# A cross-attention layer on one core: the calls to all engines issued in a new order from a table

## The chip, the cores and the metric

The kernel runs on one core of a Trainium2 chip. A core has five engines that run their own instruction queues side by side: TensorE (PE, matrix products, with its weight loads shown as PEld), VectorE (DVE), ScalarE (ACT), GpSimd (POOL) and SyncE (SP, which here only issues DMA transfers; POOL issues some too, and ACT two at the start). Each queue is worked off in its order; an instruction that waits for another engine or for a transfer holds up all that stand behind it on the same queue. The metric is the device time of one execution in microseconds (us); the time given is the median over several runs.

## The reference

Cross attention with a layer norm ahead of it and a residual behind. The masked keys of a batch get no weight; all arrays are float32.

```python
# x: (8, 256, 1024), ctx: (8, 256, 1024), mask: (8, 256), Wq, Wout: (1024, 1024), 32 heads of 32
mu = jnp.mean(hidden_states, axis=-1, keepdims=True)
var = jnp.var(hidden_states, axis=-1, keepdims=True)
x = (hidden_states - mu) * jax.lax.rsqrt(var + LN_EPS) * ln_gamma + ln_beta
Q = _split_heads(x @ Wq.T)
K = _split_heads(memory_keys)        # the context
V = _split_heads(memory_values)      # the context again
scores = jnp.einsum('bhsd,bhtd->bhst', Q, K) * scale
scores = jnp.where(mask, scores, -jnp.inf)
probs = jax.nn.softmax(scores, axis=-1)
attn = jnp.einsum('bhst,bhtd->bhsd', probs, V)
out = attn @ Wout.T                  # after the heads are joined
return residual + out
```

## The kernel before

The work is cut into 64 steps n: step n is batch n // 8 and one chunk of 128 columns (four heads of 32) of that batch's 256 rows. The names in the code carry these numbers: sc_17_2 are the scores of step 17's third head, po_0_S1 a projection of batch 0, pq_21 the query chunk of step 21.

**A step.** PE multiplies the step's queries by its keys (`scores`, L654, eight calls into four PSUM banks named sc). DVE adds the mask bias mb (L644, one per batch) and takes the row maximum (L694, e and mn); ACT takes the exponential and the row sum (L698, den); DVE takes the reciprocal (L708, rden); POOL, or ACT for some heads, scales (L714 and L712). DVE transposes e in blocks of 32 by 32 into pT (L720), ACT copies a part aside (L726, pc), and four small transfers per step, in two pairs (pT<-pT, then pT<-pc, L800, on SP), swap blocks so that pT holds the transposed weights. PE multiplies these by the values v_all (L840, pv), for most steps a pair at a time, two and three steps after the scores. ACT copies the result into at (L853).

**The projections.** The query projection of the first batches goes chunk by chunk (`make_q`, L458 and L513, pq); from batch 3 on it is done by a scheme of seven products for a two-by-two block matrix (`query_product`, L615), and so is the output projection (`product_steps`, L930, into banks named po_..., with the product's name S1, S2, A11 and so on). The schemes need sums of blocks of weights and of data: of Wout (wo, L350), of Wq (wq, ring, L564), of the normalised x (sx, L603) and of the attention (at, s2, L906), nearly all on POOL. DVE gathers the products with L636 and L631 (into qa), L972 and L968 (into r). The layer norm's gamma is folded into each chunk of Wq on POOL (L534), with a layer norm by DVE (L399 to L425) and POOL (L407), and x is transposed by PE in batch 0 (px) and by DVE and small transfers later (xe, xnT).

**What sets the order.** The loop over n issues, per step: the scores of step n + 1, output projections, values, query projections, then the softmax of step n + 1 with loads and evacuations hooked in between, then statistics, sums and folds. Where each stands is written out in the code and in a table of slots (PLAN). The scheduler is set to manual, so that each engine's queue is in the order of the calls. A buffer or PSUM bank that is written again waits for its last reader, wherever that stands.

## Time and profile before

| what | value |
|---|---|
| time, median of 3 runs | 574.21 us (573.05 to 574.57) |
| the profiled execution, first to last instruction | 572.0 us |
| PE busy | 562.9 us, 98% |
| DVE busy | 466.2 us, 81% |
| ACT busy | 450.5 us, 79% |
| POOL busy | 399.1 us, 70% |
| transfers | 116.93 MB, mean 204 GB/s |

The profiled execution's span is 2.2 us shorter than the median of the runs; differences are made within the span. In rows in order of time the first number is the start, the second the duration; `x16` means sixteen records merged into one row, and the bracket says how long the engine was idle before it and what ended that. Each float32 matmul call of the program shows as two records. A row of the waits gives the total idle time, how often, and the longest. SPq is SP issuing a transfer; the duration there is that of the issue, and the landing comes later.

### The profile page before, as it was taken

The numbers are of one execution on the slowest core, as the hardware profiler recorded it, in microseconds if no ns is written. First come the engines' busy times: TensorE is split into PE (matmuls) and PEld (weight loads), VectorE is DVE, ScalarE is ACT, GpSimd is POOL, SyncE is SP. The second block draws the span as 40 slices with busy tenths as digits, with TensorE's granted clock in tenths as the row PEclk, the third lists the DMA queues.
The fourth block names the chain that finished last, engine by engine and source line by source line (L and its number), as shares of the span: only waits on it lengthen the run. The fifth ranks groups of instructions, "written<-read, shape, count | busy, mean of one in ns | idle before, by whom it ended". The sixth has DMA issues, their size and how long they took to land.

```text
span 572.0 us, 20001 instructions
## 1 busy us (share of the span) xinstructions
PE 562.9 (98%) x7162; PEld 394.6 (69%) x7162; DVE 466.2 (81%) x1701; ACT 450.5 (79%) x1527; POOL 399.1 (70%) x643
## 2 busy tenths in 40 slices
PE   8999999999999999999999999999999999999998
PEld 7788775767667677667675777667766777755454
DVE  5988899988878888988788987898877878688833
ACT  3699978888779877888768988789868888879920
POOL 1478978887678895787667774686955875267690
PEclk9999999999999999999999999999999999999999
DMA  8768778576777677877888677767866765547551
GB/s 298 278 174 252 203 206 230 133 205 189 203 235 203 205 207 220 257 210 205 214 249 234 206 201 221 229 200 209 233 189 193 226 182 175 145 136 228 153 167 74
DMA packets 45891, 116.93 MB, mean 204 GB/s; under 512 B 9136, under 2 KB 9904, under 8 KB 45792
## 3 DMA queue, kind: packets, MB, share of 16 engines
q1 hardware_dynamic: 38080, 90.14, 55.2%
q0 software_dynamic: 7424, 25.50, 15.1%
q8 instruction: 57, 0.93, 0.7%
q14 instruction: 42, 0.34, 0.2%
q10 hardware_dynamic: 288, 0.01, 0.0%
HBM read 64.23 MB, written 11.53 MB: 132 GB/s over the span
## 4 chain that ended last, share of the span: by engine, by line
PE 69%; DVE 9%; POOL 8%; ACT 6%; issue 4%; DMA 3%; SPq 0%; DVEq 0%; ACTq 0%; POOLq 0%
PE po_S L930 17%; PE pq_A L615 16%; PE sc L654 8%; PE pv L840 8%; PE po_A L930 8%; PE pq_S L615 6%; POOL e L714 5%; ACT e L698 3%; DVE e L694 3%; PE po_end L997 3%; DVE pT L720 3%; DMA pT<-pT 2%; ACT e L712 1%; PE pq L513 1%; DMA wq<-in_wq_dram 1%
## 5 line engine op out<-in xcount | busy, mean ns | idle before, releaser
L698 ACT ACTIVATE e<-e,mn 128x256 f32<-128x256 f32 x512 | 253.7, 502 | 32.8 <-DVE mn L694 30.2
L714 POOL TENSOR_SCALAR e<-e,rden 128x256 f32<-128x256 f32 x408 | 188.5, 476 | 125.0 <-DVE rden L708 116.8
L720 DVE STREAM_TRANSPOSE pT<-e 128x512 f32<-128x512 f32 x256 | 180.4, 707 | 54.6 <-POOL e L714 23.5
L694 DVE CUSTOM_DVE_ANT_0 e<-sc,mb 128x256 f32<-128x256 f32 x512 | 185.1, 415 | 13.0 <-PE sc L654 12.0
L726 ACT COPY pc<-pT 128x512 f32<-128x512 f32 x128 | 78.8, 617 | 43.7 <-DVE pT L720 28.5
L698 ACT ACTIVATION_READ_ACCUMULATOR e<-e,mn 128x1 f32 x512 | 98.9, 193 | 0.0
L513 PE MATMUL pq<-xnT,wq 128*128 128x256 f32 (+1 forms) x368 | 84.5, 383 | 0.0
L513 PEld LDWEIGHTS pq<-xnT,wq 128*128 128x128 f32 x368 | 68.6, 190 | 14.6 <-issue 3.4
L930 PE MATMUL po_S<-wo,at 128*128 128x512 f32 x152 | 73.5, 606 | 1.0 <-DVE r L972 0.7
L654 PE MATMUL sc<-k,qa 32*128 32x256 f32 x1024 | 73.8, 401 | 0.1
L654 PEld LDWEIGHTS sc<-k,qa 32*128 32x128 f32 x1024 | 45.9, 184 | 39.0 <-issue 17.8
L840 PE MATMUL pv<-pT,v_all 64*32 64x128 f32 x3584 | 61.0, 273 | 1.0 <-ACT e L712 0.6
L840 PEld LDWEIGHTS pv<-pT,v_all 64*32 64x32 f32 x3584 | 51.9, 105 | 12.8 <-issue 7.7
L930 PE MATMUL po_A<-wo,at 128*128 128x512 f32 x128 | 59.3, 604 | 0.1
L930 PE MATMUL po_S<-wo,s 128*128 128x512 f32 x104 | 49.9, 607 | 0.3 <-DVE rden L708 0.3
L708 DVE RECIPROCAL rden<-den 128x2 f32<-128x2 f32 x256 | 37.9, 148 | 13.1 <-ACT e L698 12.1
L712 ACT ACTIVATE e<-e,rden 128x256 f32<-128x256 f32 x104 | 46.8, 500 | 1.0 <-DVE rden L708 1.0
L615 PEld LDWEIGHTS pq_A<-xnT,wq 128*128 128x128 f32 x352 | 41.1, 192 | 5.6 <-issue 4.7
L930 PEld LDWEIGHTS po_S<-wo,at 128*128 128x128 f32 x152 | 26.0, 190 | 25.7 <-issue 23.9
L694 DVE DVE_READ_ACCUMULATOR2_ANT mn<- 128x1 f32 x512 | 42.3, 83 | 0.0
L615 PE MATMUL pq_A<-xnT,wq 128*128 128x128 f32 x352 | 41.2, 275 | 0.3 <-issue 0.3
L930 PEld LDWEIGHTS po_A<-wo,at 128*128 128x128 f32 x128 | 23.0, 189 | 26.5 <-issue 24.4
(116 smaller groups left out, 687.6 us busy)
## 6 DMA issues: line engine op xcount, KB each, us to landing
pT<-pT SPq DMA_DIRECT2D x128, 128.0 KB, 3.4
pT<-pc SPq DMA_DIRECT2D x128, 128.0 KB, 4.0
v_all<-in_kv_dram POOLq DMA_DIRECT2D x17, 512.0 KB, 4.8
k<-in_kv_dram SPq DMA_DIRECT2D x30, 256.0 KB, 4.2
r<-in_x_dram SPq DMA_DIRECT2D x26, 256.0 KB, 4.0
ring<-kept_T SPq DMA_DIRECT2D x11, 512.0 KB, 5.8
xnT<-xe SPq DMA_DIRECT2D x79, 64.0 KB, 3.9
out_dram<-r POOLq DMA_DIRECT2D x18, 256.0 KB, 3.7
```

The source lines that it names most:

```text
L513: nc.tensor.matmul(pqs[n], wq[:, o, c, :], xnTs[b](c), start=(c == 0), stop=(c == NC - 1),)
L615: nc.tensor.matmul(pqs[b][:, o, :], w[:, c], x_[:, c], start=begins and o + c == 0, stop=c == NK - 1, skip_group_check=True,)
L654: nc.tensor.matmul(scs[n][j][:, s, :], qa[r, n % NQ, ts(s, P)], ks[n - n % 2][r, n % 2, :], start=True, stop=True,)
L694: nc.vector.tensor_tensor_reduce(out=e[:, s, :], in0=pss[j][:, s, :], in1=mbs[n // NQ], scale=1.0, scalar=NO_SCORE, op0=ALU.add, op1=ALU.m ...
L698: nc.scalar.activation(e[:, s, :], e[:, s, :], AF.Exp, bias=mn[:, s : s + 1], scale=-1.0, accum_out=den[:, s : s + 1],)
L708: nc.vector.reciprocal(rden, dens[j])
L712: engine.activation(es[j][:, s, :], es[j][:, s, :], AF.Copy, scale=rden[:, s : s + 1])
L714: engine.tensor_scalar(es[j][:, s, :], es[j][:, s, :], rden[:, s : s + 1], 1.0, ALU.mult, ALU.mult,)
L720: nc.vector.transpose(pT[:, :, :, j, :, :].rearrange("p a i s k -> p (a i) s k"), es[j].rearrange("p s (b t) -> p b s t", t=K),)
L726: nc.scalar.copy(pc[:, :, ts(j, 2)], pT[:, 1, :, ts(j, 2)])
L840: nc.tensor.matmul(pvs[n][r][j * HD : (j + 1) * HD], vs[n - n % 2][ts(r, 2 * K), n % 2, i, ts(j, HD)], pT[ts(r, 2 * K), :, i, j, :, :], st ...
L930: nc.tensor.matmul(po, operand(b, name)[:, c], wo[:, which, c], start=begins and c == 0, stop=c == NK - 1, skip_group_check=not begins,)
```

## The change

The 6,932 calls on the engines are no longer issued when the code makes them. A wrapper around nc records each with its arguments, numbered in the old order, and at the end issues all in the order that a table (ORDER) lists. Each call stays on its engine and in its queue (OTHER, which could move one, is empty), buffers are still allocated while recording, and all engines' instruction counts are as before. What changes is who stands before whom in each queue: 1,875 of PE's 3,613 instructions have another place, 1,530 of DVE's 1,701, 904 of ACT's 1,017, 574 of POOL's 646, 446 of SP's 478. The mean move is 2 to 6 places, the largest 138 (DVE). In the changed kernel every instruction has the line of the issuing loop, L383.

```diff
+ORDER = """
+0-35 40 38 36-37 41 39 45 42-44 54-75 77 79-82 76 78 84-93 83 94-109 120-123 134 133 111-112 110 113 118
...
+"""
+OTHER = {}
...
+class Recorder:
+    def __init__(self, engine, calls):
+        self.engine, self.calls = engine, calls
+
+    def __getattr__(self, name):
+        return lambda *a, **k: self.calls.append((self.engine, name, a, k))
+
+
+class Recorded:
+
+
+    def __init__(self, nc):
+        self.nc, self.calls = nc, []
+        for engine in ("tensor", "vector", "scalar", "gpsimd", "sync"):
+            setattr(self, engine, Recorder(engine, self.calls))
+
+    def __getattr__(self, name):
+        return getattr(self.nc, name)
+
+    def issue(self, order, other):
+
+        done = set()
+        for run in order.split():
+            first, *last = map(int, run.split("-"))
+            for i in range(first, (last[0] if last else first) + 1):
+                engine, name, a, k = self.calls[i]
+                getattr(getattr(self.nc, other.get(i, engine)), name)(*a, **k)
+                done.add(i)
+        assert len(done) == len(self.calls)
...
     ctx.enter_context(tc.manual_schedule())
+    nc = Recorded(nc)
...
+    nc.issue(ORDER, OTHER)
```

Three places, as each engine's queue has them before and after. The last number of a name counts the tiles and differs between the two kernels.

**The head, SP.** The first loads before: x_0 and x_1 are the rows of batches 0 and 1 (four pieces of x_0), wq the chunks of Wq, mk_0 the mask, k_0 the keys.

```order
L259 DMA x_0_160<-in_x_dram 128x512 x4
L334 DMA wq_152<-in_wq_dram 128x1024
L259 DMA k_0_166<-in_kv_dram 128x512
L357 DMA mk_0_168<-in_mask_dram 128x512
L259 DMA x_1_170<-in_x_dram 128x1024
L334 DMA wq_152<-in_wq_dram 128x1024
L259 DMA x_1_170<-in_x_dram 128x1024
L334 DMA wq_152<-in_wq_dram 128x1024 x3
L259 DMA k_2_177<-in_kv_dram 128x512
```

And after:

```order
L383 DMA x_0_126<-in_x_dram 128x512 x2
L383 DMA mk_0_128<-in_mask_dram 128x512
L383 DMA wq_120<-in_wq_dram 128x1024
L383 DMA x_0_126<-in_x_dram 128x512 x2
L383 DMA x_1_129<-in_x_dram 128x1024
L383 DMA k_0_127<-in_kv_dram 128x512
L383 DMA wq_120<-in_wq_dram 128x1024 x2
L383 DMA x_1_129<-in_x_dram 128x1024
L383 DMA wq_120<-in_wq_dram 128x1024
```

The last two pieces of x_0 now stand behind the mask and the first chunk of wq, and two loads of wo and the values' first load stand between chunks of wq, which k_2 now follows.

**Around the scores of step 17, PE.** s2_0 and at_0_1 are the two halves' operands of the product S1 of batch 0, which go through the same bank one after the other. Before:

```order
L930 MATMUL po_0_S1_2306<-wo_157,s2_0_1607 128x512 x4
L513 MATMUL pq_21_2311<-xnT_2_1070,wq_152 128x256 x8
L930 MATMUL po_0_S1_2306<-wo_157,at_0_1_1162 128x512 x3
L654 MATMUL sc_17_0_2401<-k_16_1958,qa_151 128x256
L654 MATMUL sc_17_1_2402<-k_16_1958,qa_151 128x256
L654 MATMUL sc_17_2_2403<-k_16_1958,qa_151 128x256
L654 MATMUL sc_17_3_2404<-k_16_1958,qa_151 128x256
L654 MATMUL sc_17_0_2401<-k_16_1958,qa_151 128x256
L654 MATMUL sc_17_1_2402<-k_16_1958,qa_151 128x256
L654 MATMUL sc_17_2_2403<-k_16_1958,qa_151 128x256
L654 MATMUL sc_17_3_2404<-k_16_1958,qa_151 128x256
L930 MATMUL po_0_S1_2306<-wo_157,at_0_1_1162 128x512
```

And after (the first half's other two matmuls stand ahead of these rows):

```order
L383 MATMUL po_0_S1_598<-wo_125,s2_0_457 128x512 x2
L383 MATMUL pq_21_599<-xnT_2_340,wq_120 128x256 x6
L383 MATMUL sc_17_0_623<-k_16_539,qa_119 128x256
L383 MATMUL sc_17_1_624<-k_16_539,qa_119 128x256
L383 MATMUL sc_17_2_625<-k_16_539,qa_119 128x256
L383 MATMUL sc_17_3_626<-k_16_539,qa_119 128x256
L383 MATMUL sc_17_0_623<-k_16_539,qa_119 128x256
L383 MATMUL sc_17_1_624<-k_16_539,qa_119 128x256
L383 MATMUL sc_17_2_625<-k_16_539,qa_119 128x256
L383 MATMUL sc_17_3_626<-k_16_539,qa_119 128x256
L383 MATMUL pq_21_599<-xnT_2_340,wq_120 128x256
L383 MATMUL po_0_S1_598<-wo_125,at_0_1_355 128x512 x4
```

The scores have moved ahead of the second half. On DVE the call that empties the bank (r_0_1_1, L972) stood behind the first transpose of step 16 (pT_16) and now stands ahead of it.

**The query product of batch 3, PE and DVE.** pq_3_A11 is one product; its sums from wq and from ring use the same bank. PE before:

```order
L615 MATMUL pq_3_A11_2964<-sx_153,wq_152 128x128 x16
L930 MATMUL po_1_S2_2772<-wo_157,at_1_1_2329 128x512 x2
L654 MATMUL sc_23_0_3225<-k_22_2762,qa_151 128x256
L654 MATMUL sc_23_1_3226<-k_22_2762,qa_151 128x256
L654 MATMUL sc_23_2_3227<-k_22_2762,qa_151 128x256
L654 MATMUL sc_23_3_3228<-k_22_2762,qa_151 128x256
L654 MATMUL sc_23_0_3225<-k_22_2762,qa_151 128x256
L654 MATMUL sc_23_1_3226<-k_22_2762,qa_151 128x256
L654 MATMUL sc_23_2_3227<-k_22_2762,qa_151 128x256
L654 MATMUL sc_23_3_3228<-k_22_2762,qa_151 128x256
L615 MATMUL pq_3_A11_2964<-sx_153,ring_105 128x128 x16
```

And after (six more of the matmuls from wq, and two of po_1_S2, stand ahead of these rows):

```order
L383 MATMUL pq_3_A11_739<-sx_121,wq_120 128x128 x2
L383 MATMUL sc_23_0_784<-k_22_705,qa_119 128x256
L383 MATMUL sc_23_1_785<-k_22_705,qa_119 128x256
L383 MATMUL sc_23_2_786<-k_22_705,qa_119 128x256
L383 MATMUL sc_23_3_787<-k_22_705,qa_119 128x256
L383 MATMUL sc_23_0_784<-k_22_705,qa_119 128x256
L383 MATMUL sc_23_1_785<-k_22_705,qa_119 128x256
L383 MATMUL sc_23_2_786<-k_22_705,qa_119 128x256
L383 MATMUL sc_23_3_787<-k_22_705,qa_119 128x256
L383 MATMUL pq_3_A11_739<-sx_121,wq_120 128x128 x8
L383 MATMUL po_1_S2_708<-wo_125,at_1_1_605 128x512 x2
L383 MATMUL pq_3_A11_739<-sx_121,ring_105 128x128 x16
```

The scores of step 23 have moved from behind the last matmul from wq into the midst of these. DVE before, at the call that gathers the product (qa):

```order
L708 RECIPROCAL rden_22_1_3191<-den_22_1_3168 128x2
L720 STREAM_TRANSPOSE pT_22_3153<-e_22_0_3155 128x8x64
L708 RECIPROCAL rden_22_2_3196<-den_22_2_3175 128x2
L720 STREAM_TRANSPOSE pT_22_3153<-e_22_1_3166 128x8x64
L708 RECIPROCAL rden_22_3_3202<-den_22_3_3186 128x2
L720 STREAM_TRANSPOSE pT_22_3153<-e_22_2_3173 128x8x64
L636 TENSOR_TENSOR qa_151<-pq_3_A11_2964,qa_151 128x4x128
L720 STREAM_TRANSPOSE pT_22_3153<-e_22_3_3184 128x8x64
```

And after:

```order
L383 RECIPROCAL rden_22_1_780<-den_22_1_772 128x2
L383 RECIPROCAL rden_22_2_781<-den_22_2_775 128x2
L383 STREAM_TRANSPOSE pT_22_765<-e_22_0_767 128x8x64
L383 ISA e_23_0_790,mn_23_0_791<-sc_23_0_784,mb_2_591 128x256
L383 ISA mn_23_0_791 128x1
L383 STREAM_TRANSPOSE pT_22_765<-e_22_2_773 128x8x64
L383 ISA e_23_2_796,mn_23_2_797<-sc_23_2_786,mb_2_591 128x256
L383 ISA mn_23_2_797 128x1
L383 ISA e_23_0_790,mn_23_0_791<-sc_23_0_784,mb_2_591 128x256
L383 ISA mn_23_0_791 128x1
L383 TENSOR_TENSOR qa_119<-pq_3_A11_739,qa_119 128x4x128
```

Ahead of qa stand now three passes of step 23's scores and two transposes of step 22; two transposes have moved behind it. Further ahead, among the score passes of step 22, DVE has the sum wq<-wq that stood after step 23's before, and it waits for a POOL sum there.

On SP's queue in steps 3 to 5, of the two loads of wo that stood between the two pairs of swaps of pT_4 one stands in the head now and one behind the swaps of pT_5; two loads of v_all, the later of which waits for the values of step 2, stand ahead of the second pair of swaps of pT_3. On POOL, folds of wq and sums of wo stand earlier between the scalings of steps 5 to 13; the fold of the last chunk of wq has a sum of wo (which stood behind it) ahead of it. At the end of the kernel the values of steps 62 and 63 follow some 5 us more of other matmuls.

## The prediction, written before the changed kernel ran

> **What bounds the kernel now.** I read the page's busy times first, then the stages, then the list of who waited for whom, and only then the order in time at the places where the waits stood. The page's two rows that matter are:

> ```profile
> PE 562.9 (98%) x7162; PEld 394.6 (69%) x7162; DVE 466.2 (81%) x1701; ACT 450.5 (79%) x1527; POOL 399.1 (70%) x643
> L714 POOL TENSOR_SCALAR e<-e,rden 128x256 f32<-128x256 f32 x408 | 188.5, 476 | 125.0 <-DVE rden L708 116.8
> ```

> TensorE is busy 98% of the span; POOL idles 125 us ahead of its scalings, some 2 us in each of 64 steps. The view by stage (span of the stage, then PE's busy time, and later the granted clock):

> ```profile
> 0.00:16.40 16.40, 13.73 (x101) 12.00 (x101) 10.31 (x30) 7.26 (x20) 2.19 (x11) 1.00 0.86 311
> 16.40:140.00 123.60, 122.61 (x1473) 91.88 (x1476) 109.04 (x407) 107.67 (x361) 99.57 (x143) 1.00 0.72 204
> 140.00:230.00 90.00, 89.33 (x1133) 62.86 (x1128) 75.82 (x271) 70.95 (x241) 68.83 (x105) 1.00 0.75 212
> 230.00:480.00 250.00, 248.43 (x3378) 177.78 (x3363) 210.19 (x778) 205.37 (x706) 179.88 (x304) 1.00 0.76 216
> 480.00:538.00 58.00, 57.90 (x807) 34.61 (x813) 45.70 (x178) 49.70 (x172) 30.82 (x57) 1.00 0.60 166
> 538.00:572.00 34.00, 30.84 (x324) 15.45 (x308) 15.12 (x40) 9.52 (x32) 17.85 (x25) 1.00 0.39 117
> ```

> PE is idle 16.40 − 13.73 = 2.7 us in the head and 3.2 us in the last stage, and 0.99 + 0.67 + 1.57 + 0.10 = 3.3 us in all the 521.6 us between. The clock is 1.00 throughout, so it has nothing to give back. An order that leaves the matmuls as they are can win only these idle times. Who ended them:

> ```profile
> PE pq_A L615 <- issue: 1.3, 2, 1.0
> PE pq L458 <- DMA wq<-in_wq_dram: 1.0, 1, 1.0
> PE po_S L930 <- DVE r L972: 0.7, 1, 0.7
> PE pv L840 <- ACT e L712: 0.6, 1, 0.6
> PE po_S L930 <- ACT ends L948: 0.3, 1, 0.3
> PE po_S L930 <- DVE rden L708: 0.3, 1, 0.3
> PE pv L840 <- DMA v_all<-in_kv_dram: 0.2, 1, 0.2
> ```

> The two "issue" gaps lie inside one query product each, with fewer matmul records there than the program has matmuls; I take them for missing records and no idle time. The other rows after the head, with one more of 0.2, sum to 2.3 us in six stalls. The true loss is a little more: a matmul's record outlasts the moment at which the next may start, so that each stall hides some 0.13 us; 2.3 + 6 × 0.13 = 3.1 us. That is all that lies in mid-kernel.

> **The change part by part.** It adds and removes nothing: each engine issues as many instructions as before, and no switch between matmul shapes is added (scores stay in groups of 8, values in their groups). PE's work is therefore costed at nothing, and every term is a stall that goes or comes.

> *The wo loads step out of pT_4's swaps.* Before:

> ```profile
> 57.69 1.12 SPq L259 DMA_DIRECT2D wo<-in_woT_dram  x2
> 58.92 1.15 SPq L800 DMA_DIRECT2D pT<-pc  x2
> 67.85 0.61 PE L840 MATMUL pv<-pT,v_all 64*32 64x128 f32 x19 [0.61 <-ACT e L712]
> ```

> The wait is booked to ACT's e, which had long been done; the values of step 4 need the swapped block, whose second pair was issued behind 1 MB of wo. Without that MB (half of it is loaded in the head now, half after pT_5's swaps, both well ahead of wo's use) the swap lands in time, and this stall (0.6, or 0.7 from start to start) goes.

> *The evacuation before the second half of po_0_S1.* Before:

> ```profile
> 144.53 3.62 PE L513 MATMUL pq<-xnT,wq 128*128 128x256 f32 x16
> 148.11 0.65 DVE L972 TENSOR_TENSOR r<-po_S,r 128x512 f32<-128x512 f32 x1
> 148.81 0.70 PE L930 MATMUL po_S<-wo,at 128*128 128x512 f32 x1 [0.67 <-DVE r L972]
> ```

> The bank must be emptied (0.65 us on DVE) before PE writes it again. DVE's queue held that call behind a transpose; now it stands before the transpose, and PE has scores of 17 (some 1.1 us) among its work in between. This stall, the largest, goes: 0.8.

> The other four (v_all of step 6 is loaded earlier, the end's evacuations have more PE work ahead of the next use) make up the rest. Removed in all: −3.1, with the ends −3.1 and −1.5 (only these two).

> *The head.* SP's queue loads the second half of x_0 behind the mask and the first 512 KB of wq; before, it stood ahead of both. The rows of before, with the traffic between 2.5 and 8.5 us:

> ```profile
> 7.85 0.69 DVE L399 BATCH_NORM_STATS2 st<-x 128x6 f32<-128x512 f32 x1 [0.19 <-DMA x<-in_x_dram]
> 9.24 2.02 PE L458 MATMUL pq<-xnT,wq 128*128 128x128 f32 x16 [1.04 <-DMA wq<-in_wq_dram]
> 9.91 0.80 DVE L425 TENSOR_SCALAR x<-x,mv,rstd 128x1024 f32<-128x1024 f32 x1
> 15.72 0.31 PEld L654 LDWEIGHTS sc<-k,qa 32*128 32x128 f32 x8 [0.48 <-ACT qa L462]
> 2.50:8.50 6.00, 5.51 (x36) 5.04 (x34) 3.81 (x7) 1.98 (x3) 0.58 (x1) 1.00 0.95 299
> ```

> 576 KB at 299 GB/s are 1.9 us; the transfers overlap, so x_0's end comes 1.1 to 1.9 us later, and the chain statistics, norm (9.91), transposes, projection, scores (15.72) with it. Against that, wq comes as much earlier, and the wait of 1.04 at 9.24 goes: PE can do the first half's projection while it waits for the second half. DVE also has two statistics of x_1 (0.69 each) before the copies of x_0. From −1.0 (only the wq wait moves) to +1.9 (the whole delay). I take +0.75, above the middle, since the second half feeds the chain that ends last in this stage.

> *pT_3's second pair of swaps* now stands behind two loads of v_all, the later of which waits until the values of step 2 have read their buffer.

> ```profile
> 49.97 1.15 SPq L800 DMA_DIRECT2D pT<-pc  x2
> 52.09 1.16 PE L840 MATMUL pv<-pT,v_all 64*32 64x128 f32 x64
> 59.63 0.63 PE L840 MATMUL pv<-pT,v_all 64*32 64x128 f32 x26
> pT<-pc SPq DMA_DIRECT2D x128, 128.0 KB, 4.0
> pT<-pc SPq DMA_DIRECT2D x3, 128.0 KB, 7.0
> ```

> So it is issued at 52.09 + 1.16 + one load's issue (0.5), about 53.8 to 54.9 instead of 49.97 to 51.1. A swap lands after 4.0 us in the page's median and after 7.0 in the crowded stretch from 56 to 69 us. The block is wanted at 59.63: 58.9 is in time, 61.9 is 2.3 too late. There is less traffic now that wo has gone elsewhere, so I stay near the low end: +0.4 (0 to +2.3). Behind this wait on SP stand pT_4's swaps, issued from 56.2 on before; they are not reached.

> *POOL's fillers* (folds of wq, sums of wo) move ahead of scalings. Their cover is POOL's idle time above. Where there is none is the last fold:

> ```profile
> 84.53 1.90 POOL L534 TENSOR_TENSOR wq<-wq,gs 128x1024 f32<-128x1024 f32 x1
> 86.38 1.28 POOL L350 TENSOR_TENSOR wo<-wo 128x512 f32<-128x512 f32 x1
> 86.48 0.51 PEld L513 LDWEIGHTS pq<-xnT,wq 128*128 128x128 f32 x3 [0.38 <-POOL wq L534]
> ```

> The fold ends at 86.43, 0.05 us before its use. The sum of 1.28 behind it now stands ahead of it, inside step 8's scalings: 0 if those scalings wait less than they did, +1.2 if not. I take +0.3, by the 2 us that POOL idles in a step.

> *Query products.* In batch 3 the scores of 23 move out from between two groups of pq_3_A11 that share a bank:

> ```profile
> 202.88 1.88 PE L930 MATMUL po_S<-wo,at 128*128 128x512 f32 x4
> 204.44 0.65 DVE L636 TENSOR_TENSOR qa<-pq_A,qa 128x512 f32<-128x512 f32 x1
> 205.77 0.49 PE L615 MATMUL pq_A<-sx,ring 128*128 128x128 f32 x2
> ```

> PE left the bank at 202.88 and came back at 205.77. Now only the projection's matmuls are in between (202.88 to 204.70: 1.8), and DVE's sum of 0.65 must fit: room 1.8 − 0.65 = 1.2. DVE began it 204.44 − 202.88 = 1.6 late before, which would now cost 0.4. The queue order gives DVE two transposes ahead of it instead of three, but three score passes too. Batches 5 and 7 have the same gap, 4 and 6 a longer one. I take +0.3 for the three (0 to 3 × 0.4 = +1.2).

> The rest of the moved calls I cost at nothing. What hides them is that a step's values are computed two or three steps after its scores, which the order keeps: from 230 to 480 us PE lost 1.57 us, 1.3 of them the issue gaps, though the swaps, loads and evacuations of 30 steps were queued there. Where that cover is gone, a late pair of swaps costs what pT_3's does.

> Sum: −3.1 + 0.75 + 0.4 + 0.3 + 0.3 = −1.35, against 572.0 of span. The median of the runs, 574.21, is 2.2 above the span, which I leave: 574.21 − 1.35 = 572.9, say **572.8**. Its own range is 571.1 (the head at −1.0, the rest as taken) to 574.5 (only the two large stalls gone).

> **Rivals.** *Everything gained, nothing paid:* the wq wait gives 1.0 in the head and no new stall comes: 574.2 − 3.1 − 1.0 = 570.1. For it: PE's idle time in the head; against it: the x_0 chain. *Even:* the toll is twice what I took (2 × 1.75 = 3.5) and the gain 3.1: 574.6, within the ±0.3% (±1.7 us) that a measurement of this kernel can tell from no change. For it: 98% busy leaves nothing else.

> *Slower:* DVE held up by POOL at the query products. Two sums of the same form on DVE, and POOL beside the slow one:

> ```profile
> 142.14 1.32 POOL L564 TENSOR_TENSOR ring<-wq 128x512 f32<-128x512 f32 x1
> 142.26 1.75 DVE L564 TENSOR_TENSOR ring<-wq 128x512 f32<-128x512 f32 x1
> L564 DVE TENSOR_TENSOR wq<-wq x2: 650/664/678, 160.7 to 213.9; 128x512 f32<-128x512 f32 x2
> ```

> Beside POOL's sum the 0.65 became 1.75, 1.1 more; the new order puts one such sum (213.9 before) ahead of step 22's reciprocals, where it waits for POOL and meets its sums. If DVE is as late at pq_A as before (1.6) and 1.1 more, PE waits 2.7 − 1.2 = 1.5; with the same lateness in batches 3, 5 and 7, 4.5, and so 572.8 − 0.3 + 4.5 = 577.0. It decides from the point where DVE is over 1.2 us late. Against it: DVE idles ahead of the same sum now. [...]

> **How the numbers follow.** Forecast 0.48, half of it beyond the bound (0.24 faster, 0.24 same); everything gained 0.13; even 0.08; slower 0.31, in which I count pT_3's swaps at their upper end too. Faster 0.24 + 0.13 = 0.37; same 0.32; slower 0.31. The range goes from 570.0, the full gain, to 578.0, the slower rival's 577.0 with a little of a late fold; it leaves about 0.15 out.

> **What would show it.** Right: no wait of po_S for r L972 near 148 and none of pv near 67; PE's first unbroken stretch beginning 0.5 to 1 us later than 16.4; pq at 86 waiting for wq under 0.5. Wrong: a wait of pv near 60 for pT<-pc over 1 us; pq_A waiting for qa in batches 3, 5, 7; idle time on PE between 230 and 480 above 2 us, where I expect no new wait; or a switch of shape costing more in another neighbourhood, seen as PE busy above 563.

## The result, and the profile after

The changed kernel takes 581.91 us (median; 580.96 to 584.02) against 574.15 (573.05 to 574.57): a ratio of 1.0157, 95% interval 1.0126 to 1.0187. It is slower, by more than the forecast's range allowed. The profiled execution spans 579.3 us against 572.0, 7.3 more, and the working below is made on these two. One run of e1 (712.28 us, at a mean granted clock of 0.754) is left out of the figures below. The page of after, its busy times:

```profile
PE 565.7 (98%) x7162; PEld 400.4 (69%) x7162; DVE 459.6 (79%) x1701; ACT 451.8 (78%) x1527; POOL 402.0 (69%) x643
```

The view by stage, cut as in the prediction (the last stage is longer now):

```profile
0.00:16.40 16.40, 10.90 (x61) 10.50 (x62) 7.51 (x16) 3.52 (x7) 2.19 (x11) 0.90 0.85 301
16.40:140.00 123.60, 123.60 (x1417) 92.26 (x1415) 107.88 (x417) 108.72 (x364) 106.64 (x148) 1.00 0.72 209
140.00:230.00 90.00, 90.00 (x1146) 64.91 (x1146) 74.46 (x272) 70.60 (x237) 60.92 (x95) 1.00 0.75 209
230.00:480.00 250.00, 245.27 (x3393) 177.38 (x3392) 202.24 (x757) 203.18 (x697) 173.37 (x297) 1.00 0.74 210
480.00:538.00 58.00, 57.46 (x724) 35.85 (x728) 46.53 (x177) 47.22 (x164) 35.88 (x61) 1.00 0.63 181
538.00:579.30 41.30, 38.42 (x430) 19.53 (x424) 20.98 (x67) 18.50 (x63) 22.98 (x33) 1.00 0.37 108
```

PE is idle 16.40 − 10.90 = 5.5 us in the head (2.7 before), not at all from 16.4 to 230 (1.7 before), 4.7 from 230 to 480 (1.6 before), 0.5 to 538 (0.1) and 2.9 at the end (3.2). That is 4.5 more in all, and PE is busy 565.7 − 562.9 = 2.8 longer for the same matmuls: together the 7.3. Two stages got worse and the one between them got better. Who ended the waits:

```profile
PE pq L383 <- DVE xnT L383: 2.8, 1, 2.8
PE pq_A L383 <- issue: 2.2, 2, 1.2
PE pv L383 <- DMA pT<-pc: 1.7, 3, 0.9
PE busy L383 <- POOL ring masks.py:199: 1.3, 1, 1.3
PE pq L383 <- DMA wq<-in_wq_dram: 1.3, 1, 1.3
PE sc L383 <- DMA k<-in_kv_dram: 0.8, 1, 0.8
```

The waits of po_S for r, of pv for ACT's e, for v_all and so on are gone, as forecast. In their place stand x_0's copies in the head, the swaps of pT and a load of keys.

To see where the time is lost, I take each matmul call's start in a trace and subtract the time at which it would start if every call took as long, up to the start of the next, as in the kernel before. This "lag" is my own working from two traces, one execution of each kernel; it rises where PE loses time and falls where a stall of before is missing. The kernels of this document that are told apart by it (the edits of e1 to e16 are given with the experiments):

| lag in us at | 20 | 220 | 240 | 360 | 480 | 560 |
|---|---|---|---|---|---|---|
| after | 4.6 | 2.2 | 5.1 | 5.1 | 7.0 | 7.0 |
| e1 (x_0 first) | 1.3 | −0.9 | 2.0 | 1.7 | 5.1 | 4.9 |
| e8 (copies first) | 2.3 | 0.1 | 4.6 | 5.8 | 7.4 | 7.1 |
| e7 (PE kept busy in the head) | 3.1 | 0.7 | 3.4 | 4.2 | 8.3 | 8.4 |
| e15 (old order, first twelve loads new) | 2.1 | 6.5 | 6.5 | 5.5 | 9.2 | 9.1 |
| e11 (first twelve loads as before) | 0.3 | −1.3 | 1.2 | 0.8 | 3.7 | 3.4 |
| e9 (as e11 up to step 21, then the old order) | 0.0 | −2.4 | −2.4 | −2.0 | −1.7 | −1.7 |
| e10 (as e11, swaps in pairs) | 0.3 | −1.6 | 1.0 | 0.6 | 6.6 | 7.2 |
| e16 (as e11, three late places mended) | 0.3 | −1.7 | 3.2 | 2.9 | 6.7 | 7.3 |
| e13 (as e11, ScalarE's copies early) | 0.2 | −0.5 | −0.4 | 4.1 | 15.2 | 18.9 |

After loses 4.6 us by 20 us, wins 2.4 back up to 220, and loses 4.8 from there on, 2.9 of them between 220 and 240.

**The head.** The first statistics of x_0's second half on VectorE (DVE) in before:

```profile
6.97 0.69 DVE L399 BATCH_NORM_STATS2 st<-x 128x6 f32<-128x512 f32 x1
```

The rows of after in order of time, DVE first:

```profile
10.07 1.36 DVE L383 BATCH_NORM_STATS2 st<-x 128x6 f32<-128x512 f32 x2 [3.25 <-DMA x<-in_x_dram]
...
11.83 0.41 DVE L383 TENSOR_SCALAR xnT<-px,gam,bet 128x128 f32<-128x128 f32 x1
12.77 0.73 DVE L383 TENSOR_SCALAR xnT<-px,gam,bet 128x128 f32<-128x128 f32 x2 [0.53 <-ACT xnT L383]
```

and PE:

```profile
9.51 0.91 PE L383 MATMUL pq<-xnT,wq 128*128 128x128 f32 x6 [1.33 <-DMA wq<-in_wq_dram]
13.23 2.50 PE L383 MATMUL pq<-xnT,wq 128*128 128x128 f32 x10 [2.82 <-DVE xnT L383]
15.53 1.38 PE L383 MATMUL px<-ring,x 128*128 128x128 f32 x8
16.84 0.71 PE L383 MATMUL sc<-k,qa 32*128 32x256 f32 x8
```

The statistics of x_0's second half begin at 10.07, in before at 6.97. In DVE's queue the copies of the *first* half (xnT<-px), whose transposes PE ended near 8.2 us, stand behind those statistics, so that they too begin only at 11.83, and PE, which could have projected the first half, waits 2.82 us. The three copies stood behind the statistics before, too, but their own order is new: the one that PE needs next was the first of them and is now the second, behind another and behind a copy of ACT's from the same px (12.28 to 12.73), for which DVE waits 0.53 us. From the first copy's start to PE's next matmul it takes 13.23 − 11.83 = 1.40 us. In e15, which has these loads with the old order of the copies, it takes 0.47 (11.19 to 11.66). So some 0.9 of the 2.82 us come from the order of the copies. Then the matmuls run slowly: ten in 2.50 us. The clock in the view by stretches of 2 us:

```profile
12.00:14.00 2.00, 0.77 (x3) 0.77 (x4) 1.47 (x5) 0.46 (x1) 0.85 (x3) 0.70 1.02 406
14.00:16.00 2.00, 2.00 (x12) 2.00 (x11) 1.62 (x3) 0.22 (x1) 0.00 (x0) 0.50 1.03 400
16.00:18.00 2.00, 2.00 (x19) 1.50 (x18) 1.05 (x4) 1.54 (x5) 0.00 (x0) 0.94 1.05 394
```

By the trace's clock records the granted clock is 0.50 from 12.81 us, near the end of the wait, to 16.23. In before it was 1.00 in every stretch of 2 us up to 570, where PE's last matmul was over.

**After 220 us.** SP's queue, whose rows give the issue, and PE:

```profile
223.51 4.12 SPq L383 DMA_DIRECT2D pT<-pc  x2
227.67 0.98 SPq L383 DMA_DIRECT2D k<-in_kv_dram  x1
...
231.12 0.51 SPq L383 DMA_DIRECT2D pT<-pT  x1
231.68 0.58 SPq L383 DMA_DIRECT2D pT<-pc  x1
```

```profile
231.37 1.78 PE L383 MATMUL sc<-k,qa 32*128 32x256 f32 x16 [0.83 <-DMA k<-in_kv_dram]
235.19 1.25 PE L383 MATMUL pv<-pT,v_all 64*32 64x128 f32 x64 [0.95 <-DMA pT<-pc]
```

The load of k_26 is issued at 227.67 behind swaps (218.89 before). The last swap of pT_23 is issued at 231.68 behind a swap of the *next* step; the copy that feeds it had ended at 219.4. In the old order each step's four swaps stand in two unbroken pairs ahead of the next step's; in the new one 20 of 64 steps have a swap behind the next step's first, and 19 have one to seven other transfers inside the second pair. The life of two steps, from the traces (us):

| step | | last score | last transpose | last copy | last swap issued | values begin |
|---|---|---|---|---|---|---|
| 23 | before | 205.8 | 213.4 | 214.1 | 223.2 | 230.2 |
| 23 | after | 204.6 | 217.8 | 219.4 | 232.3 | 235.2 |
| 44 | before | 384.2 | 392.2 | 392.8 | 399.3 | 417.2 |
| 44 | after | 386.7 | 400.2 | 408.0 | 415.0 | 421.7 |

From the last score to the last swap it took 17.4 and 15.1 us before, and takes 27.7 and 28.3 now: every engine on the way hands on later. From the last swap's issue to the values there were 7 and 18 us; 3 and 7 are left, with a wait of PE in them both times.

The two steps are ones at whose values PE waits. By the same working for steps 24 to 59, the median from the last score to the last swap is 14.7 us before and 23.1 after, and from there to the values 12.5 and 6.8. Less than 5 us are left in none of these 36 steps before, in 13 of them after, and in none in e9, which has the old order there. In steps 4 to 19 the median has shrunk as much, from 12.9 to 6.5, and PE loses nothing there.

### The profile page after: what moved, and what is told of

It is laid out like the page before. It is cut to its first block, busy times and chain, and to the rows that moved or that the text cites. A ratio compares the mean times of both kernels' runs of the same rounds, so it can differ in the third digit from the quotient of the medians.

```text
span 579.3 us, 19950 instructions
## 1 busy us (share of the span) xinstructions
PE 565.7 (98%) x7162; PEld 400.4 (69%) x7162; DVE 459.6 (79%) x1701; ACT 451.8 (78%) x1527; POOL 402.0 (69%) x643
## 4 chain that ended last, share of the span: by engine, by line
PE 71%; DMA 9%; DVE 7%; ACT 4%; issue 3%; SPq 3%; POOL 2%; DVEq 0%; POOLq 0%; ACTq 0%
PE pq L383 15%; PE po_S L383 13%; PE sc L383 9%; PE pv L383 9%; PE pq_A L383 8%; PE po_A L383 7%; PE pq_S L383 5%; DMA pT<-pc 4%; DMA pT<-pT 3%; SPq L383 3%; ACT e L383 3%; PE po_end L383 3%; DVE e L383 2%; DVE pT L383 2%; POOL e L383 2%
## 5 line engine op out<-in xcount | busy, mean ns | idle before, releaser
L383 ACT ACTIVATE e<-e,mn 128x256 f32<-128x256 f32 x512 | 256.1, 503 | 43.5 <-DVE mn L383 33.3
L383 POOL TENSOR_SCALAR e<-e,rden 128x256 f32<-128x256 f32 x408 | 191.9, 482 | 131.3 <-DVE rden L383 126.8
L383 DVE STREAM_TRANSPOSE pT<-e 128x512 f32<-128x512 f32 x256 | 176.9, 702 | 32.7 <-POOL e L383 22.6
L383 DVE CUSTOM_DVE_ANT_0 e<-sc,mb 128x256 f32<-128x256 f32 x512 | 192.8, 411 | 12.2 <-PE sc L383 6.6
L383 ACT ACTIVATION_READ_ACCUMULATOR e<-e,mn 128x1 f32 x512 | 97.5, 190 | 0.0
L383 PE MATMUL pq<-xnT,wq 128*128 128x256 f32 (+3 forms) x400 | 92.7, 380 | 4.2 <-DVE xnT L383 2.8
L383 ACT COPY pc<-pT 128x512 f32<-128x512 f32 x128 | 77.3, 613 | 21.8 <-DVE pT L383 12.9
L383 PEld LDWEIGHTS pq<-xnT,wq 128*128 128x128 f32 x400 | 72.7, 194 | 23.2 <-issue 8.9
L383 PE MATMUL sc<-k,qa 32*128 32x256 f32 x1024 | 75.7, 401 | 0.8 <-DMA k<-in_kv_dram 0.8
L383 PE MATMUL po_S<-wo,at 128*128 128x512 f32 x152 | 72.6, 597 | 0.0
L383 DVE RECIPROCAL rden<-den 128x2 f32<-128x2 f32 x256 | 37.6, 153 | 43.3 <-ACT e L383 42.0
L383 PEld LDWEIGHTS sc<-k,qa 32*128 32x128 f32 x1024 | 47.8, 184 | 27.7 <-issue 14.3
L383 PE MATMUL pv<-pT,v_all 64*32 64x128 f32 x3584 | 60.7, 273 | 1.8 <-DMA pT<-pc 1.4
L383 PE MATMUL po_A<-wo,at 128*128 128x512 f32 x128 | 61.2, 602 | 0.0
L383 PEld LDWEIGHTS pv<-pT,v_all 64*32 64x32 f32 x3584 | 51.4, 105 | 13.4 <-issue 7.8
L383 ACT ACTIVATE e<-e,rden 128x256 f32<-128x256 f32 x104 | 49.2, 502 | 6.3 <-DVE rden L383 5.9
L383 PEld LDWEIGHTS pq_A<-xnT,wq 128*128 128x128 f32 x352 | 42.9, 192 | 12.3 <-issue 10.6
L383 PE MATMUL po_S<-wo,s 128*128 128x512 f32 x104 | 50.4, 601 | 0.0
L383 PE MATMUL pq_A<-xnT,wq 128*128 128x128 f32 x352 | 44.4, 277 | 1.2 <-issue 1.2
L383 DVE DVE_READ_ACCUMULATOR2_ANT mn<- 128x1 f32 x512 | 42.4, 83 | 0.0
L383 ACT COPY at<-pv 128x128 f32<-128x128 f32 x128 | 30.5, 252 | 13.9 <-PE pv L383 13.9
L383 PEld LDWEIGHTS po_S<-wo,at 128*128 128x128 f32 x152 | 26.1, 191 | 18.7 <-issue 18.3
## 6 DMA issues: line engine op xcount, KB each, us to landing
pT<-pT SPq DMA_DIRECT2D x128, 128.0 KB, 3.3
pT<-pc SPq DMA_DIRECT2D x128, 128.0 KB, 3.6
```

The costliest lines, as they stand in the source:

```text
L383: getattr(getattr(self.nc, other.get(i, engine)), name)(*a, **k)
```

## The experiments

Ratios are to the kernel before, run on the same chip. Each kernel is the changed one with its table edited. The numbers are those of calls: 34 to 37 are x_0's loads, 38, 42 and 44 to 46 wq, 39 k_0, 40 the mask, 41 and 43 x_1.

### The head mended in three ways

e1 puts x_0's second half back behind the first:

```diff
-0-35 40 38 36-37 41 39 45 42-44 54-75 77 79-82
+0-37 40 38 41 39 45 42-44 54-75 77 79-82
```

> The new order with one edit on SP's queue: the last two pieces of x_0 again right behind the first two, ahead of the mask and the first piece of wq. Theory A (the head's loss is this load: x_0's second half lands 2 us late, DVE's queue holds the copies of the first half behind its statistics, PE idles 2.8 us and then runs 1.4 us longer at a lower clock): about 4.5 us less than the new order, 577.4, with pq_0 waiting under 0.5 us and the clock at 1.00 from 12 to 18 us. Theory B (the pace is set by the other engines' chains, so what the head gives is waited away at the first late swap): less than 1.5 us gained, 580.5 or more, with longer waits of pv in steps 3 to 10.

580.86 us, 1.0125 (1.0088 to 1.0161). e8 leaves the loads and puts the copies of the first half (79, 76, 78) ahead of the second half's statistics (60 to 63) on DVE:

```diff
-54-75 77 79-82 76 78 84-93
+54-59 65-75 77 79-82 76 78 60-64 84-93
```

> The new order with one edit on DVE's queue: the three copies of x_0's transposed first half stand ahead of the statistics of its second half (and the pool's power that follows them behind POOL's two small copies). SP's loads stay as in the new order. Theory A (the copies were held up by statistics that waited for the load): the wait of 2.8 us in pq_0 goes, the second half's own wait of 1 to 2 us comes in its place, and the clock does not fall: 2 to 3.5 us less than the new order in the head. If the late load alone counted, under 1 us.

581.74 us, 1.0132 (1.0093 to 1.0172). e7 fills the head's wait with 15 transposes of the identity on PE, work that the reference does not have, so as to keep the clock up:

```diff
-    for _ in range(32):
+    for _ in range(47):
         nc.tensor.transpose(busy, ident, ident)
```

> The new order as it is, with 15 more transposes of the identity on PE (as those it does while it waits for the first loads) in the place in pq_0 where PE idles 2.8 us; they add work and change no other order. If the matmuls behind the idle stretch were slow because PE had been idle: granted clock 1.00 from 12 to 18 us and a head 1.2 to 1.5 us shorter than in the new order, 580.0 to 580.8 against 581.9. If the low clock came from anything else: no gain, or up to 0.3 us lost by work that runs past the wait.

583.41 us, 1.0141 (1.0084 to 1.0199). PE's rows of e7, and its clock:

```profile
13.09 1.38 PE L383 MATMUL pq<-xnT,wq 128*128 128x128 f32 x10 [1.18 <-DVE xnT L383]
...
15.35 0.71 PE L383 MATMUL sc<-k,qa 32*128 32x256 f32 x8
```

```profile
14.00:16.00 2.00, 2.00 (x22) 1.45 (x20) 2.00 (x5) 1.26 (x4) 0.00 (x0) 1.00 1.01 394
```

The ten matmuls take 1.38 instead of 2.50, and the scores begin at 15.35 instead of 16.84: from 13.1 to here the slow clock cost 1.35 us. All three mend what they were to mend (lag at 20 us 1.3 in e1, 2.3 in e8, 3.1 in e7), and by the runs none of the three is told from the changed kernel. By the lag e1 keeps 2.1 of the 3.3 us that it wins in the head, e8 and e7 keep nothing: in e8 the lag rises from 0.1 to 4.6 between 220 and 240. Behind 220 us e1 loses 5.8, e8 7.0 and e7 7.7 us. So there is a second cause.

### Old and new order joined in time

Kernels that begin in the one order and go on in the other: e2 has the old order for the first 254 calls, e4 up to step 21, and the new one behind; e3 has the new order from call 254 to step 21, old before and behind.

```diff
-0-35 40 38 36-37 41 39 45 42-44 ...
+0-253 326 287 489 597 388 254-262 270 ...
```

> All calls up to the scores of step 1 in the old order, the rest in the new one. Theory A: as with x_0 alone, 577 to 577.8, since nothing else in the head costs. Theory B: 580.5 or more. If it comes out over 1 us below the run with x_0 alone, something else in the head (k_2 behind more bytes, DVE's statistics of x_1) costs as well.

> Old order up to the scores of step 1, the new one from there to the scores of step 21, the old one for the rest. Theory A: the new order gains its four old stalls here (2.4 us by the lag between the two traces) and pays only later: 571.5 to 572.2, faster than both. Theory B: the new order is slower at each step by small waits that do not show as PE idle: 574.5 or more.

> Old order up to the scores of step 21, the new one from there on. Theory A: only the new waits behind late swaps and late keys after 220 us: 574.2 + 4 to 5 = 578.2 to 579.2, with the keys of step 26 and the swaps of step 23 waited for. Theory B (these waits come from a backlog that the new order built up earlier): under 576.

587.39 us, 1.0236 (1.0194 to 1.0277); 580.27, 1.0126 (1.0080 to 1.0171); 590.55, 1.0305 (1.0269 to 1.0341). None can be read by its total: each has a wait at the seam itself, where the engines change orders at different points. There PE waits once for DVE to empty a bank of scores, 4.8 us in e2, 6.5 in e3 and 7.6 in e4. With the slow clock behind them (0.89 from 30 to 60 us in e2 and e3, 0.92 from 140 to 230 in e4) these cost 8 to 12 us of lag, so the totals say nothing of the two orders. What can be read is the lag away from the seam. In e3 it falls by 2.5 from 60 to 220 us; behind that, in the old order, it stays within 0.5 up to 355 us and then rises by 1.6 at two gaps that no engine ends. In the new order behind 220 us it rises by 6.0 in e2, and by 2.7 in e4, behind its wait of 7.6.

e9 avoids the seam at the head, with the first twelve loads as before (calls 34 to 45; the expectations count eleven) and the new order from there on, up to step 21:

```diff
-0-35 40 38 36-37 41 39 45 42-44 54-75 ...
+0-45 54-75 ...
...
+2205-2206 2208 2212-2213 2249-2252 2254-2294 2296-6931
```

> The new order with the first eleven loads of SP's queue as in the old order, up to the scores of step 21; the old order from there on. By the two parts seen so far (the head at most 0.5 us behind the old, the stalls of the new order's first 200 us gone, the old order's rest without the waits after 220 us): 2 to 2.5 us under the old kernel of the same chip, 571 to 571.6 where it has 573.5. If the place where the orders meet costs a wait, as it did in the three cut orders before, it is more by that wait.

573.14 us, 0.9988 (0.9962 to 1.0013), not told from the kernel before; the profiled execution is 570.4 against 572.0. PE's waits in it have no pv waiting for a swap and no sc for a load. In these single executions the new order is better than the old one up to 220 us, by 2.4 us of lag, and the loss lies in what follows; the runs do not tell the gain from none.

### All loads back at their old places

e5: x_0 first, and every other load and store of SP at its old place among the swaps; all else new.

```diff
 SP: calls that are no swaps
-    where the new table has them
+    behind as many swaps as in the old order
```

> The new order with x_0 loaded first and, on SP's queue, every load and store other than the swaps of pT back behind as many swaps as stood ahead of it in the old order; the other engines as in the new order. Theory C (the waits after 220 us come from loads that stand ahead of swaps on SP's queue and hold them up): no wait of sc for k near 228 and of pv for pT near 232; the 5.9 us that the kernel with x_0 first loses after 220 us fall below 2, 573 to 575.5. Theory D (ACT's and DVE's new order makes the copies late, and SP only passes it on): 577.5 or more, with the same steps waiting.

683.13 us, 1.187 (1.1809 to 1.1931). PE, DVE and POOL now ask in the new order for what SP brings in the old one; pq_A alone waits for POOL's e 13.9 us at one place and 16.3 in sum for stored sums. It tells nothing of the cause, only that the queues' orders belong together.

### The head alone, both ways

e11 is the new order with the first twelve loads as before, e15 the old order with the first twelve as in the new one.

```diff
 e11
-0-35 40 38 36-37 41 39 45 42-44 54-75 ...
+0-45 54-75 ...
 e15
-0-6931
+0-35 40 38 36-37 41 39 45 42-44 46-6931
```

> The new order with one thing undone: the first eleven loads on SyncE's queue stand as before (x_0 whole, then the weights, k_0, the mask and x_1). This is the head repaired alone, and the control for the next run. If the head alone makes the change slower (lag of 4.6 us at 20 us, all from x_0 and wq): TensorE at 20 us is level with the kernel before (0 +- 0.3), the time is 574 to 577. If the pace behind 220 us is set by the late swaps of the transposed probabilities, what the head gains is waited away there: lag about -2 at 220 us, then waits of pv for pT<-pc of 3 us or more in sum, and 577 to 580.

> The kernel before, with nothing moved but SyncE's first twelve loads, which stand in the new order. If the head costs by itself what the trace of the changed kernel shows (2.8 us of waiting for x_0's second half, 1.3 for wq, and the slow clock after it): TensorE lags 4 to 5 us at 20 us and keeps that to the end, 578 to 580. If the old order has room that takes it up (the prediction's way): 574 to 575.5.

e11: 577.59 us, 1.0063 (1.0041 to 1.0085). e15: 578.47 us, 1.0086 (1.0053 to 1.0119). The head makes 1.57 − 0.63 = 0.94% of the loss, some 5.4 us, when its loads are put back in the new order. The 0.86% of e15 is close to it by luck. In e15's trace the head's wait is 1.6 us, the clock stays at 1.00 and the lag is 2.1 at 20 us: with all else in the old order, the copies too, the same loads cost less than half of the 4.6. The fastest of its six executions, 576.00, is 1.5 above the median of before. The rest of the profiled one, the slowest of the six, is mostly pv waiting for v_all, once for a load that took 10.7 us to land, which I leave unexplained:

```profile
PE pv L216 <- DMA v_all<-in_kv_dram: 4.1, 2, 2.5
...
PE pq L216 <- DVE xnT L216: 1.6, 1, 1.6
```

What e11 keeps, 0.63%, less e9's −0.12%, is the part behind step 21: 0.75%, some 4.3 us. By the lag e11 loses 4.7 there, from −1.3 at 220 us to 3.4, and e9 0.7, mostly at gaps that no engine ends, so that 4.0 are left. Why e1, with only 1.0 more lag at 20 us, is 0.6% slower than e11 is not settled; in part it is the clock, whose mean was 1.000 in five of e11's eight executions (575.92 to 577.90 us) and in one of these three of e1.

### What makes the transfers late behind 220 us

e10 is e11 with the swaps of each step in unbroken pairs, ahead of the next step's first swap.

```diff
 SP, step 23, with what stood in between
-pT_23<-pc  k_26  xnT  out_0  xnT  k_28  pT_24<-pT  pT_23<-pc
+pT_23<-pc  pT_23<-pc  k_26  xnT  out_0  xnT  k_28  pT_24<-pT
```

> As the run before it, and on SyncE's queue the four swaps of each step are put back into two pairs without a gap, both ahead of the first swap of the next step (in the new order 20 of 64 steps have a swap of their last pair behind the next step's first swap, and 19 have one to eight other transfers inside that pair). If the split pairs make the late waits: pv's waits for pT<-pc fall under 0.5 us in sum and the time is 573 to 575, 2 us or more under the run before it. If the copies on ScalarE that feed the swaps are themselves late (the rival), the waits stay within 1 us of the run before it, and so does the time.

580.20 us, 1.0110 (1.0072 to 1.0147). No row of pv waiting for a swap is left, but the first row of PE's waits is

```profile
PE sc L383 <- DMA k<-in_kv_dram: 3.3, 2, 2.1
```

The wait went from the swaps to the loads behind them in the same queue, and the median is above e11's. The one execution of e10 whose clock stayed at 1.000 took 577.20 us, no more than e11's. The split pairs are not the cause by themselves.

e13 is e11 with 63 of ScalarE's copies (L726 of the code before) earlier in its queue, and e14 has that and the pairs.

```diff
 ACT, step 44
-e_45 x2  its scalings x2  e_45  xnT x2  pc_44  ...
+pc_44  e_45 x2  its scalings x2  e_45  xnT x2  ...
```

> As the run with the first eleven loads put back, and on ScalarE 63 copies of transposed probabilities (steps 20 to 63) stand one to thirteen calls earlier, ahead of the first call that began after their transposes were done; SyncE's queue is that of the control. In the control these copies wait 166 us in sum behind other calls of ScalarE after their transposes are done, 2.6 us each. If the late copies are the cause: the late waits of pv for pT<-pc and of sc for k fall from some 2.5 to under 1 us, and the time is 573.5 to 576 against the control's 577.6. If they are late for another reason (the rival: VectorE's transposes, or SyncE's own order): within 1 us of the control.

> As the run before it, and the swaps of each step in unbroken pairs ahead of the next step's first swap. With copies that come early the pairs should no longer hold up the k loads behind them: if copies and swaps together are the cause, 572 to 575 and no wait of pv for pT<-pc; if the swap pairs only push the wait to the k loads whatever the copies do (as in the run of pairs alone, 580.2), 578 or more.

e13: 590.89 us, 1.0303 (1.0281 to 1.0325); e14: 584.65 us, 1.0177 (1.0154 to 1.0199). Both are misses: copies that come earlier do not mend the loss. They do not show that late copies cost nothing, since other calls of ACT now come later in their place. The waits of PE and of DVE (DVE from 220 to 560 us) in e13:

```profile
PE sc L384 <- DVE mn L384: 4.4, 3, 3.1
```

```profile
DVE rden L384 <- ACT e L384: 39.5, 52, 4.6
```

With copies ahead, ACT's exponentials come later, DVE's reciprocals wait for them, the score passes behind these in DVE's queue come late, and PE waits for a bank.

e12 has PE's calls alone in the new order and all other engines' in the old one.

```diff
 PE
-the old order
+the new order
 DVE, ACT, POOL, SP
 the old order
```

> TensorE's calls alone in the new order; VectorE, ScalarE, GpSimd and SyncE issue all of theirs in the order of before, loads and swaps included. If the loss comes from the other queues (late loads, split swaps): no head wait for x_0, no late wait for pT<-pc above 0.5 us in sum, and the time is 571 to 575. If TensorE's own new order asks for values before anybody could have them (the rival): waits of pv or po of 2 us or more in sum remain, and 577 or more.

600.90 us, 1.0488 (1.0444 to 1.0531). The rival's outcome. The waits of pv that it named are there, and others that it did not name, the largest of pq_A for ACT:

```profile
PE pq_A L370 <- ACT xnT L370: 5.1, 1, 5.1
PE pv L370 <- DMA v_all<-in_kv_dram: 3.4, 4, 1.6
PE pq_A L370 <- POOL wq L370: 2.8, 1, 2.8
```

PE's new order asks for things sooner than the old queues bring them. It needs the other engines' new orders.

e16 is e11 with seven calls moved, at the three places where its trace shows PE waiting for a late transfer.

```diff
 SP
-pT_23<-pT  pT_22<-pc  pT_23<-pc  k_26  xnT ... pT_24<-pT  pT_23<-pc
+k_26  pT_23<-pT  pT_22<-pc  pT_23<-pc  pT_23<-pc  xnT ... pT_24<-pT
 ACT: the two copies pc_44 ahead of the last two exponentials of step 45
 SP: the last three swaps of pT_44 behind its first
```

> As the run with the first eleven loads put back (577.6), and seven calls a few places earlier: on SyncE the load of k_26 and the last swap of pT_23, on ScalarE the two copies of pc_44, on SyncE the last three swaps of pT_44. If the late loss is these places: the waits of sc_26 for k_26 (0.5 to 1.3 us), pv_23 (0.9) and pv_44 (1.0) go, nothing takes their place, lag at 440 us about -1, and the time is 574.5 to 575.5. If the new order is narrow everywhere, so that each call moved up pushes another late (the rival): those three waits go and others come, and the time is within 1 us of 577.6 or above.

580.74 us, 1.0104 (1.0059 to 1.0149): the rival's outcome. The three waits are gone, and this stands in their place (SP, ACT, DVE, PE of e16):

```profile
218.27 0.65 SPq L382 DMA_DIRECT2D k<-in_kv_dram  x1
218.97 1.18 SPq L382 DMA_DIRECT2D pT<-pT  x1
220.19 6.41 SPq L382 DMA_DIRECT2D pT<-pc  x3
```

```profile
226.51 1.14 ACT L382 COPY pc<-pT 128x512 f32<-128x512 f32 x2 [4.76 <-DMA pT<-pc]
```

```profile
229.16 0.17 DVE L382 RECIPROCAL rden<-den 128x2 f32<-128x2 f32 x1 [4.30 <-ACT e L382]
```

```profile
229.71 1.13 PE L382 MATMUL sc<-k,qa 32*128 32x256 f32 x10 [2.65 <-DVE mn L382]
```

This is the chain in one view. The copies of a step write one of two buffers (the pool asp has two), which the swaps of the step but one before must have read. pT_22's last swap, the first of the three issued from 220.19, now stands behind the 256 KB of k_26 and lands at 226.41 (225.14 in e11); ACT's copy begins at 226.51, 4.76 us after ACT was free, with exponentials queued behind it; DVE waits 4.30 for an exponential, with the scores' pass queued behind its reciprocal; PE waits 2.65 for the bank. (In e11 the same copy waits 3.10 us and PE 0.39.) That a third buffer would cut this chain at its first link is an estimate from these rows; it was not tried. Of the 3.9 us by which e16's lag ends above e11's, up to 3.4 are two stretches of 3.41 us in which the granted clock is 0.50, the first behind this wait (from 230.81), the second behind a gap that no engine ends (from 479.99).

How this differs from before shows in DVE's waits from 220 to 560 us. Before:

```profile
DVE pT L720 <- ACT e L712: 12.5, 17, 1.6
DVE e L694 <- PE sc L654: 11.6, 12, 2.4
DVE rden L708 <- ACT e L698: 8.9, 13, 1.0
```

After:

```profile
DVE rden L383 <- ACT e L383: 29.0, 38, 2.8
...
DVE pT L383 <- ACT e L383: 5.3, 10, 1.2
DVE e L383 <- PE sc L383: 4.0, 7, 1.1
```

Before, DVE waited for PE: the softmax chain was ahead of the matmuls, and PE's queue was the one that set the pace. Now its reciprocals wait three times as long for ACT (its transposes less, 5.3 for 12.5), and its passes over the scores wait a third as long for PE: the chain is about level with PE, and a hitch in it can reach PE. Mending one call only moved the hitch, in e10, e13, e14 and e16. That the narrow spacing as a whole is what costs the 0.75% is the reading that all of these fit; no run widens the spacing and keeps the new order, so it is not shown. Which of its moves brought it about was not isolated.

## Why the prediction was wrong

**The stalls that go (−3.1): right in kind, 2.4 in size.** No po_S waits for r near 148, no pv near 67; PE does not stop once from 16.4 to 230 us. The lag falls by 2.4 from 20 to 220 us in after, and the steps in it stand where they were forecast: −0.7 at pT_4's values, −0.7 at po_0_S1. e9's profiled execution keeps 1.7 of it; its runs are not told from before.

**The head (+0.75, at most +1.9): mis-sized; it measured 4.6.** Four things were wrong in it. x_0's second half came later than its bound: the statistics that read it begin 10.07 − 6.97 = 3.1 us later, not 1.1 to 1.9. The sentence "PE can do the first half's projection while it waits for the second half" fails by DVE's queue: the copies that this projection needs stand behind the second half's statistics. The order of before had shown it (the copies at 8.94 behind the statistics at 7.85), and the prediction read PE's queue only. The new order of the copies among themselves, some 0.9 us, was not seen. And nothing was put in for the clock, which cost 1.35. The wait for wq did not go either; it is 1.33 instead of 1.04. By the runs of e11 against after this step is 0.9%, some 5 us, where 0.75 was taken.

**"The rest of the moved calls I cost at nothing": the step that failed.** The reason given was that a step's values are computed two or three steps after its scores, "which the order keeps". It does keep that. But the cover is not the distance in steps; it is what is left of it after every engine has handed on later, and of the 12.5 us from the last swap to the values in the median of steps 24 to 59 only 6.8 were left. The prediction had 1.57 us of idle time on PE between 230 and 480 and took it as proof of slack, without looking at how early each queue's work was done. What is lost there is 4.8 us of lag in after, 0.75% by e11 and e9. That this cover is what the loss came from is the reading that fits, not a thing isolated.

**The issue gaps ("missing records and no idle time"): wrong.** No record is missing: two for each of PE's 3,549 float32 products and one for each of its 64 transposes are the page's 7,162, and they stand in the order of the calls. The lag is about 1.1 lower behind 275 us in the new orders, where the gap of before at 269.67 is absent, and it rises for good by 0.8 near 357 and by 1.1 near 480, at two gaps that before does not have there: +0.8 net in after. They are lost time in these executions. They do not belong to the new order: e9 and e3, with the old order there, lose 0.7 and 1.3 us net behind 220, mostly at such gaps. What makes them is open.

**pT_3's swaps, the last fold, the query products (+0.4, +0.3, +0.3): nothing came.** PE has no wait at 60 us, at 86 us or for qa in batches 3, 5 and 7. The rival by which POOL holds DVE up at the query products did not occur: it took 1.75 us for a sum on DVE, from one of before, and the sum that it names (wq<-wq, 213.9 before) took 0.86 in after (at 200.81), with POOL at sums from 199.85 to 202.80. Its time, 577.0, is of the right sign by the wrong mechanism.

**The signs that were named:** PE idle over 2 us from 230 to 480 (4.7) and PE busy above 563 (565.7) both came. The second was tied to a switch of shape. About half of the 2.8 (1.35) is the slow clock of the head.

By the lag: head +4.6, the stalls that go −2.4, k_26 and pv_23 +2.9, issue gaps +0.8, later values (pv_28 0.7, pv_44 0.5, pv_57 and pv_58 0.9, less small gains) some +1.3: together 7.2, against 7.3 of span.

## What to carry to other kernels

An order is worth what its queues have in reserve, not what the busiest engine idles: before a reordering is costed at nothing, measure for each step how long its result lies ready before it is used, on every engine of the chain, and see whether the engines wait for the bound engine or for one another. For a call that comes later, look at what is queued behind it on its own engine, whether or not that needs it: two loads moved behind two others cost 2.1 us here, and 4.6 with the copies in another order, through copies that do not read them. And mend such an order as a whole (here by keeping only its first 220 us): in all four tries here single moves passed the wait on.

## What the runs showed of the hardware

In e10 PE waits 2.11 us for keys, until 417.77; the stretches behind the wait:

```profile
417.70:419.50 1.80, 1.73 (x56) 1.38 (x64) 0.55 (x3) 0.02 (x1) 1.80 (x4) 0.93 0.60 132
419.50:421.50 2.00, 2.00 (x90) 2.00 (x83) 1.91 (x6) 0.58 (x2) 2.00 (x3) 0.50 0.92 293
```

The issue gaps of 1 to 2 us keep their places in the program: in after, e10, e11, e13 and e16 they stand ahead of the product pq_5_A11 and within some 4 us of pq_7_A11, in before inside pq_4_A11. e9, with the old order behind step 21, has one there too (266.67), and one of 0.99 us near 351. Neither an engine nor a transfer is shown as ending them.
